# Gated cross-attention and mixture block: value diagonals copied in four steps, another softmax order, six score banks in batch 0

## The chip, the cores and the metric

The kernel runs on one core of a Trainium2 chip. The metric is the device time of one execution in microseconds (us), as the median of several runs. All data is float32.

## The reference

A decoder block works on x, of shape 8 batches x 256 tokens x 512, and on a context of the same shape.

```python
x = x + tanh(g_xattn) * attention(layernorm(x), context)      # 32 heads of 16, 8 key/value heads
x = x + tanh(g_ffn)   * feed_forward(layernorm(x))            # 128 experts, 4 chosen, plus a shared one
```

In the attention the queries come from the context and x together (1024 to 512). There are two sets of keys and values, one from the context and one from x, each with 8 heads. A token sees the 64 latest positions in each set, with a linear bias by distance and one softmax over both sets. A projection Wo follows.

In the feed-forward part all experts share 8 basis networks (512 to 256, silu(gate) * up). An expert is a mixture of them by its amplitudes, so that a token needs the 8 basis results, weighted by coefficients from the 4 experts that its router chose, then one product with w_down. A shared network of width 512 is added.

## The kernel before, in words

**Work and stages.** A batch has 256 tokens, two tiles of 128. Four kinds of work exist for each batch b, each a Python generator: `project(b)` (queries, keys, values; `project_first` for batch 0), `attention(b)`, `tail(b, t)` (Wo, layer norm, router, for token tile t) and `feed_forward(b)`. The code of all engines is emitted in one order: `run` (L1076) always resumes the generator whose planned time is earliest, and a `yield c` moves it on by c times a rate. Each engine, and each DMA queue, then executes its share strictly in the order of emission. In the middle of the run the feed-forward of batch b lies beside the attention of b+1 and the projection of b+2. Batch 0's attention has no feed-forward beside it, only `project(1)`.

**Attention.** `attention(b)` (L499) works on 8 groups i of two query blocks of 32 tokens; step u = 2i + j is block j of group i. `score(i)` (L515) writes the scores of group i into four PSUM banks, one for each pair p of key/value heads, by 8 matmuls. A bank has 512 columns: 192 for j = 0, 192 for j = 1, and the last 128 for results of `values`. At each step u, VectorE runs `soften` for the four pairs (bias and row minimum, L540), ScalarE the exponentials (L554), then, a step later, `divide` (reciprocal on VectorE, L563, scaling on GpSimd, L566), and two steps later `turn` transposes the probabilities (L574). `values(m, s, ...)` (L579) multiplies the probabilities of four steps with the values; it runs at the two steps of groups 3, 5, 7 and 9, right behind the scores, and writes into the last columns of the banks of pairs 0 and 1 of that same group. `take` (L609) copies them out on ScalarE. The work of a step is emitted in three pieces with a `yield` between them (L652): pair 0, pair 1, then pairs 2 and 3.

**Banks.** Of the eight PSUM banks, `ps_sc` has four in rotation (scores), `ps_gu` three, named gu0, gu1 and gu2 (feed-forward, by `next_bank`, in rotation), and `ps_one` one. `tail` uses `ps_one` once the feed-forward of batch 0 has been started, and `next_bank` before that.

**Values and diagonals.** `put_values` (L411) copies the values of a batch to `vpad`. For `values` they must stand in blocks on the diagonals of `vbd`. This is done by 16 DMAs of 128 KB on the queue of SyncE (SP), L628 to L634, all emitted at the start of step u = 3 for batch 0 and of step u = 1 for the others.

**The SP queue.** SP also issues nearly all other transfers, in order: x and the context of the batch after next (L105, L111), and the feed-forward weights (`load_gu`, L286). In batch 0 the feed-forward forms sums and differences of the weights (`sub`, L801: L805 and L807 on VectorE, L809 and L810 on GpSimd) and stores them in HBM (`keep`, L812, L814), from where later batches read them. In iteration k of the eight basis networks, each weight block for k + 2 is loaded as soon as the matmuls that used its buffer are emitted (`after`, L308). Differences of iteration k + 1 are formed in iteration k.

Of the kernel before, what the change touches and what calls it, by code (L numbers as in the profile page):

```python
# [36 lines left out]
def gated_block(  # L37
# [41 lines left out]
    def next_bank(name):  # L79
        turns[0] += 1  # L80
        return ps_gu.tile([P, 2, T], F32, tag=f"gu{turns[0] % 3}", name=name)

# [243 lines left out]
    def project_first():  # L328

        xt, ctT = loaded[0]  # L330
        xnT = two.tile([P, NC, T], F32, tag="xo", name="xnT_0")
        kT = two.tile([P, 2, 2, T], F32, tag="kT", name="kT_0")
        qT = two.tile([P, NB, G, Q], F32, tag="qT", name="qT_0")
        tiles = [slice(t * P, (t + 1) * P) for t in range(NT)]

        def early(name, parts):
            bank = ps_sc.tile([P, 512], F32, tag="sc", name=name)
            return bank.rearrange("p (a n) -> p a n", a=parts)

        def keys(pk, s, cols):  # L340
            w_sb, src = ((wsk_sb, ctT), (wk_sb, xnT))[s]
            for c in range(NC):
                nc.tensor.matmul(
                    pk[:, s, cols], lhsT=w_sb[:, c, :], rhs=src[:, c, cols],
                    start=(c == 0), stop=(c == NC - 1),
                )

        def put_keys(pk, s, cols):
            for par in range(2):
                nc.scalar.activation(  # L350
                    kT[:, par, s, cols], pk[:, s, cols], AF.Copy, scale=kmask[:, par : par + 1]
                )

        def queries(pq, g, cols, cs):
            for c in cs:
                nc.tensor.matmul(
                    pq, lhsT=wq_sb[:, c, g * P : (g + 1) * P],
                    rhs=(ctT if c < NC else xnT)[:, c % NC, cols],
                    start=(c == 0), stop=(c == 2 * NC - 1),
                )  # L360

        def put_queries(pq, g, t):
            blocks = slice(t * NB // NT, (t + 1) * NB // NT)
            nc.scalar.activation(
                qT[:, blocks, g, :], pq.rearrange("p (b q) -> p b q", q=Q), AF.Copy, scale=-0.25
            )

        pk = early("pk_0", 2)
        keys(pk, 0, slice(0, T))
        pqs = [next_bank(f"pq_0_{g}")[:, 0, :P] for g in range(G - 1)]  # L370
        pqs.append(ps_one.tile([P, P], F32, tag="one", name="pq_0_3"))
        for g in range(G):
            queries(pqs[g], g, tiles[0], range(NC))
        put_keys(pk, 0, slice(0, T))
        transposed(xnT, first_normed[0], 0, "x0", lambda shape, name: early(name, NC))()
        keys(pk, 1, tiles[0])
        for g in range(G):
            queries(pqs[g], g, tiles[0], range(NC, 2 * NC))
        put_keys(pk, 1, tiles[0])
        for g in range(G):  # L380
            put_queries(pqs[g], g, 0)
        projected[0] = kT, qT
        yield 0.0
        evict = transposed(
            xnT, first_normed[1], 1, "x0",
            lambda shape, name: next_bank(name).rearrange("p t (a n) -> p (t a) n", n=P),
        )
        yield 0.5
        evict()
        pk = next_bank("pk_0_1")  # L390
        keys(pk, 1, tiles[1])
        yield 0.6
        put_keys(pk, 1, tiles[1])
        pv = next_bank("pv_0").rearrange("p t (s n) -> p t s n", s=2)
        for t in range(NT):
            for s, (w_sb, src) in enumerate(((wsv_sb, ctT), (wv_sb, xnT))):
                for c in range(NC):
                    nc.tensor.matmul(
                        pv[:, t, s, :], lhsT=src[:, c, tiles[t]], rhs=w_sb[:, c, :],
                        start=(c == 0), stop=(c == NC - 1),  # L400
                    )
            yield 1.0
        put_values(pv)
        ready.add("values")
        for g in range(G):
            pq = next_bank(f"pq_0_{g}_1")[:, 0, :P]
            queries(pq, g, tiles[1], range(2 * NC))
            yield 1.0
            put_queries(pq, g, 1)

    def put_values(pv):  # L411
        nc.scalar.copy(
# [86 lines left out]
    def attention(b):  # L499
# [11 lines left out]
        def seen(row, qb):  # L511

            return row.rearrange("p (s k) -> p s k", s=2)[:, :, max(0, NW - 1 - qb) * Q :]

        def score(i):  # L515

            par, qb0 = groups[i]
            scs = [
                ps_sc.tile([P, 2 * COLS + P], F32, tag="sc", name=f"sc_{b}_{i}_{p}")
                for p in range(NPAIR)  # L520
            ]
            for j in range(2):
                qb = qb0 + j
                first = max(0, qb - NW + 1)
                for p in range(NPAIR):
                    rows = slice(32 * p, 32 * (p + 1))
                    nc.tensor.matmul(  # L527
                        seen(scs[p][:, j * COLS : (j + 1) * COLS], qb),
                        lhsT=qT[rows, qb].rearrange("p g q -> p (g q)"),
                        rhs=kT[rows, par, :, first * Q : (qb + 1) * Q],  # L530
                        start=True, stop=True,
                    )
            return scs
# [86 lines left out]
        prs, dens, pts = {}, {}, {}  # L620
        for u in range(2 * n + 4):
            i, j = divmod(u, 2)
            if u == (1 if b > 0 else 3):
                while "values" not in ready:
                    yield 0.2


                for qd in range(P // Q):  # L628
                    for g in range(G):
                        at = D * (1 - g % 2)  # L630
                        nc.sync.dma_start(
                            vbd[g * Q : (g + 1) * Q, qd].rearrange("p a k r -> p a (k r)"),
                            vpad[qd * Q : (qd + 1) * Q, :, at : at + 2 * HK * D],
                        )  # L634
            m = i // 2 - 1 if i >= 3 and i % 2 else None
            if j == 0:
                if i < n:
                    scs = score(i)
                elif m is not None:
                    scs = [  # L640
                        ps_sc.tile([P, 2 * COLS + P], F32, tag="sc", name=f"sc_{b}_{i}_{p}")
                        for p in range(2)
                    ]
            if m is not None:
                values(m, j, pts[m], scs)
            exponentials()
            if i < n:
                prs[u] = three.tile([P, NPAIR, COLS], F32, tag="pr", name=f"pr_{b}_{u}")
                nmax = small.tile([P, NPAIR], F32, tag="nmax", name=f"nm_{b}_{u}")
                dens[u] = small.tile([P, NPAIR], F32, tag="den", name=f"dn_{b}_{u}")  # L650
            yield 1.0
            for step, ps in enumerate(((0,), (1,), (2, 3))):  # L652
                exponentials()
                for p in ps:
                    if i < n:
                        soften(i, j, p, scs, prs[u], nmax, dens[u])
                if step == (0 if b > 0 else 1) and 0 <= u - 1 < 2 * n:
                    divide((u - 1) // 2, (u - 1) % 2, prs[u - 1], dens.pop(u - 1))
                if step == (1 if b > 0 else 2) and 0 <= u - 2 < 2 * n:
                    k = (u - 2) // 4  # L660
                    if (u - 2) % 4 == 0:
                        pts[k] = two.tile(
                            [P, P // Q, NPAIR, COLS], F32, tag="pt", name=f"pt_{b}_{k}"
                        )
                    turn(u - 2, prs.pop(u - 2), pts[k])
                if step == 1 and j == 1 and m is not None:
                    take(m, scs)
                    if m == n // 4 - 1:
                        start(tail(b, 0, oT), 0.30 if b > 0 else 0.22, total=37.0)
                if u < 2 * n + 2:  # L670
                    yield 1.0 if i < n else 0.8
# [22 lines left out]
    def tail(b, t, oT):  # L694
# [1 line left out]
        mine = []  # L696

        def take_bank():
            mine.append("fed" in ready)
            if mine[-1]:  # L700
                yield from hold()

# [4 lines left out]
        def bank(shape, name):  # L707
            if mine[-1]:
                return ps_one.tile(shape, F32, tag="one", name=name)
            flat = next_bank(name).rearrange("p a n -> p (a n)")[:, : prod(shape[1:])]  # L710
            return flat.rearrange("p (a n) -> p a n", a=shape[1]) if len(shape) == 3 else flat

        n = f"{b}_{t}"
# [443 lines left out]
```

## Time and profile before

| what | value |
|---|---|
| median of 3 runs (lowest, highest) | 1052.18 us (1050.83, 1053.58) |
| profiled execution, its own time | 1053.74 us |
| its span in the profile | 1051.8 us |
| TensorE (PE) busy | 1002.5 us, 95% |
| PE weight loads busy | 797.0 us, 76% |
| VectorE (DVE) busy | 583.4 us, 55% |
| ScalarE (ACT) busy | 422.6 us, 40% |
| GpSimd (POOL) busy | 428.6 us, 41% |
| DMA traffic | 177.13 MB, mean 168 GB/s |

The profile is one execution. Views used below: the busy time of each engine in chosen stretches of the span, with the TensorE clock that was granted (1.00 is full speed) and the share of the DMA engines in use; the waits, which say who waited for whom; and the timeline of one engine, in which a bracket at the end of a line gives the idle time ahead of the instruction and what ended it. On the SP queue's timeline an entry is the issue of a transfer, not its landing. A count of PE matmuls in the trace is twice that of the program, since a float32 matmul shows as two.

### The profile page before, as it was taken

Reading aid. Unit: us, or ns where it says so; the run is one execution under the profiler, and the core shown is the slowest. Engines: PE = TensorE matmul, PEld = TensorE weight load, DVE = VectorE, ACT = ScalarE, POOL = GpSimd, SP = SyncE. Lnnn points to the kernel's source line nnn. Section 1 sums busy time; section 2 is a strip of 40 time slices with the busy share of each in tenths; the row PEclk is TensorE's granted clock in tenths of the full one; section 3 lists DMA queues with packets and bytes.
Section 4 is the critical chain, followed back from the end, with each engine's and each line's share of the span. In section 5 each row is a group of like instructions: output and inputs, shape, how many; then the busy total and the mean of one; then the engine's idle time right before and its main releaser. Section 6 shows DMA issues by size and latency. Waiting matters only on the chain.

```text
span 1051.8 us, 26704 instructions
## 1 busy us (share of the span) xinstructions
PE 1002.5 (95%) x10072; PEld 797.0 (76%) x10072; DVE 583.4 (55%) x2193; ACT 422.6 (40%) x1608; POOL 428.6 (41%) x844
## 2 busy tenths in 40 slices
PE   6779959999999999999999999999999999999998
PEld 5656848786878778886878868787787868777885
DVE  1554657656754465635755367554665457654452
ACT  3542425425643255423644155432554236531220
POOL 3333558623643145531654136441455215640340
PEclk9879989999999999999999999999999999999999
DMA  8700685537745485436844387453864457653780
GB/s 251 196 15 4 173 257 160 169 99 210 249 135 158 122 264 177 141 112 175 279 128 162 101 227 227 129 170 107 257 193 132 129 155 236 193 172 111 260 281 20
DMA packets 109856, 177.13 MB, mean 168 GB/s; under 512 B 11936, under 2 KB 34976, under 8 KB 109728
## 3 DMA queue, kind: packets, MB, share of 16 engines
q1 hardware_dynamic: 107616, 173.59, 54.2%
q10 hardware_dynamic: 2112, 1.84, 0.5%
q8 instruction: 79, 1.29, 0.5%
q14 instruction: 49, 0.40, 0.1%
HBM read 146.02 MB, written 12.58 MB: 151 GB/s over the span
## 4 chain that ended last, share of the span: by engine, by line
PE 78%; DVE 6%; issue 2%; ACT 1%; ACTq 0%; DVEq 0%
PE m L857 30%; PE ps L991 11%; PE pq L469 8%; PE pd L1054 5%; PE sc L596 5%; PE po L721 5%; PE sc L527 4%; PE pd L1037 3%; PE pv L489 2%; PE pk L450 2%; DVE pr L540 1%; PE pl L752 1%; DVE pt L574 1%; DVE st_a L150 1%; ACT pr L554 1%
## 5 line engine op out<-in xcount | busy, mean ns | idle before, releaser
L566 POOL TENSOR_SCALAR pr<-pr,rd 128x192 f32<-128x192 f32 (+2 forms) x512 | 209.3, 427 | 301.6 <-DVE rd L563 301.6
L554 ACT ACTIVATE pr<-pr,nm 128x192 f32<-128x192 f32 (+2 forms) x512 | 218.6, 430 | 141.1 <-DVE nm L540 80.0
L857 PE MATMUL m<-w,sT 128*128 128x256 f32 x1024 | 254.2, 382 | 11.4 <-DVE th L825 11.4
L540 DVE CUSTOM_DVE_ANT_1 pr<-sc,nbias 128x192 f32<-128x192 f32 (+2 forms) x512 | 153.5, 322 | 158.3 <-PE sc L596 84.5
L857 PEld LDWEIGHTS m<-w,sT 128*128 128x128 f32 x1024 | 195.4, 192 | 38.9 <-DVE th L825 11.8
L857 PE MATMUL m<-w,hT 128*128 128x256 f32 x768 | 204.1, 388 | 0.0
L857 PEld LDWEIGHTS m<-w,hT 128*128 128x128 f32 x768 | 139.9, 191 | 24.5 <-issue 5.6
L930 POOL TENSOR_TENSOR mixed<-mixed,th 128x256 f32<-128x256 f32 x112 | 82.2, 734 | 161.5 <-DVE th L925 155.5
L991 PE MATMUL ps<-hT,w 128*128 128x256 f32 x512 | 117.6, 381 | 0.0
L574 DVE STREAM_TRANSPOSE pt<-pr 128x768 f32<-128x768 f32 (+2 forms) x128 | 111.5, 871 | 3.4 <-POOL prob L761 2.8
L991 PEld LDWEIGHTS ps<-hT,w 128*128 128x128 f32 x512 | 95.2, 190 | 14.6 <-issue 2.9
L554 ACT ACTIVATION_READ_ACCUMULATOR pr<-pr,nm 128x1 f32 x512 | 97.6, 191 | 0.0
L596 PEld LDWEIGHTS sc<-pt,vbd 64*32 64x32 f32 x5120 | 60.6, 106 | 24.6 <-issue 15.1
L527 PE MATMUL sc<-kT,qT 32*128 32x192 f32 (+2 forms) x1024 | 68.5, 343 | 7.9 <-DVE nm L540 4.8
L596 PE MATMUL sc<-pt,vbd 64*32 64x96 f32 (+2 forms) x5120 | 68.8, 228 | 5.5 <-DMA vbd<-vpad 3.3
L527 PEld LDWEIGHTS sc<-kT,qT 32*128 32x128 f32 x1024 | 48.9, 188 | 29.5 <-issue 8.6
L893 POOL TENSOR_TENSOR m<-m,u 128x256 f32<-128x256 f32 x64 | 47.3, 739 | 58.6 <-DVE u L892 50.4
L820 ACT ACTIVATE th<-m 128x256 f32<-128x256 f32 x64 | 24.6, 385 | 98.1 <-DVE up L903 98.1
L469 PE MATMUL pq<-ctT,wq 128*128 128x256 f32 x224 | 55.9, 394 | 3.1 <-ACT kT L457 2.9
L721 PE MATMUL po<-wo,oT 128*128 128x512 f32 x128 | 58.2, 597 | 0.0
L915 DVE TENSOR_TENSOR gate<-u,m 128x256 f32<-128x256 f32 x64 | 26.2, 409 | 55.0 <-PE m L857 55.0
L469 PE MATMUL pq<-xnT,wq 128*128 128x256 f32 x224 | 54.9, 389 | 0.0
(130 smaller groups left out, 1179.8 us busy)
## 6 DMA issues: line engine op xcount, KB each, us to landing
w<-s SPq DMA_DIRECT2D x224, 256.0 KB, 3.2
w<-in_L_ffn_w_gate SPq DMA_DIRECT2D x128, 256.0 KB, 3.0
w<-in_L_ffn_w_up SPq DMA_DIRECT2D x72, 256.0 KB, 3.9
vbd<-vpad SPq DMA_DIRECT2D x128, 128.0 KB, 3.0
s<-w SPq DMA_DIRECT2D x32, 256.0 KB, 3.3
w<-in_L_ffn_shared_w_gate SPq DMA_DIRECT2D x32, 256.0 KB, 3.1
w<-in_L_ffn_shared_w_up SPq DMA_DIRECT2D x32, 256.0 KB, 2.8
ctT<-in_ctx SPq DMA_DIRECT2D x8, 512.0 KB, 5.8
```

The source lines that it names most:

```text
L469: nc.tensor.matmul(pq, lhsT=wq_sb[:, c, g * P : (g + 1) * P], rhs=(ctT if c < NC else xnT)[:, c % NC, :], start=(c == 0), stop=(c == 2 * N ...
L527: nc.tensor.matmul(seen(scs[p][:, j * COLS : (j + 1) * COLS], qb), lhsT=qT[rows, qb].rearrange("p g q -> p (g q)"), rhs=kT[rows, par, :, f ...
L540: nc.vector.tensor_tensor_reduce(out=part, in0=seen(scs[p][:, j * COLS : (j + 1) * COLS], qb0 + j), in1=bass.AP(tensor=bias.tensor, offset ...
L554: nc.scalar.activation(part, part, AF.Exp, bias=nmax, scale=-1.0, accum_out=den)
L566: nc.gpsimd.tensor_scalar(part, part, rden[:, p : p + 1], 1.0, op0=ALU.mult, op1=ALU.mult)
L574: nc.vector.transpose(pt[:, u % 4].rearrange("p c (s k) -> p (c s) k", s=2)[:, :, lo:], pr.rearrange("p c (s k) -> p (c s) k", s=2)[:, :, ...
L596: nc.tensor.matmul(scs[gp][32 * c : 32 * (c + 1), 2 * COLS + lo * Q : 2 * COLS + hi * Q], lhsT=vbd[rows, kb % (P // Q), kb // (P // Q) * 2 ...
L721: nc.tensor.matmul(po, lhsT=oT[:, ch // 2, ch % 2, t * P : (t + 1) * P], rhs=wo_sb[:, ch % 2, ch // 2, :], start=(ch == 0), stop=(ch == 3),)
L857: nc.tensor.matmul(dst, lhsT=sides_of[m][c], rhs=w[:, c, :], start=(first and c == 0), stop=(c == NC // 2 - 1), skip_group_check=True,)
L930: nc.gpsimd.tensor_add(mixed[t], mixed[t], th)
L991: nc.tensor.matmul(pg[:, j, :], lhsT=w[c // 2][:, c % 2, ic % 2 * P : (ic % 2 + 1) * P], rhs=hT[:, c, :], start=(c == 0), stop=(c == NC - 1),)
L1054: nc.tensor.matmul(po, lhsT=lhsT, rhs=rhs, start=False, stop=(j == len(inner) - 1))
```

## The change

Four things change.

1. The 16 diagonal copies become a function, `diagonals(qd)`, of four DMAs. Batch 0 calls it four times directly behind `put_values`. The other batches call it once in each of four places: at the first and second piece of steps u = 1 and u = 2.
2. A step treats its pairs in the order 2, 3, then 0 and 1. The scores are computed in the same order of pairs.
3. From group 4 on, batch 0's scores rotate over six banks: the four of `ps_sc`, gu0 and gu1. The first four groups, and all groups of other batches, keep the four.
4. Batch 0's tails, where they used `next_bank`, use one fixed bank: gu2 for token tile 0 and gu0 for tile 1.

```diff
+    def other_bank(n, name):
+        return ps_gu.tile([P, 2 * T], F32, tag=f"gu{n}", name=name)
...
         put_values(pv)
-        ready.add("values")
+        for qd in range(P // Q):
+            diagonals(qd)
         for g in range(G):
...
+    def diagonals(qd):
+        for g in range(G):
+            at = D * (1 - g % 2)
+            nc.sync.dma_start(
+                vbd[g * Q : (g + 1) * Q, qd].rearrange("p a k r -> p a (k r)"),
+                vpad[qd * Q : (qd + 1) * Q, :, at : at + 2 * HK * D],
+            )
...
+        taken = [0]
+        def bank(name):
+            taken[0] += 1
+            if b == 0 and taken[0] > 4 * NPAIR and taken[0] % 6 < 2:
+                return other_bank(taken[0] % 6, name)
+            return ps_sc.tile([P, 2 * COLS + P], F32, tag="sc", name=name)
+
         def score(i):
...
-            scs = [
-                ps_sc.tile([P, 2 * COLS + P], F32, tag="sc", name=f"sc_{b}_{i}_{p}")
-                for p in range(NPAIR)
-            ]
+            scs = [bank(f"sc_{b}_{i}_{p}") for p in range(NPAIR)]
...
-                for p in range(NPAIR):
+                for p in (2, 3, 0, 1):
...
-            if u == (1 if b > 0 else 3):
-                while "values" not in ready:
-                    yield 0.2
-                for qd in range(P // Q):
-                    for g in range(G):
-                        at = D * (1 - g % 2)
-                        nc.sync.dma_start(
-                            vbd[g * Q : (g + 1) * Q, qd].rearrange("p a k r -> p a (k r)"),
-                            vpad[qd * Q : (qd + 1) * Q, :, at : at + 2 * HK * D],
-                        )
...
-            for step, ps in enumerate(((0,), (1,), (2, 3))):
+            for step, ps in enumerate(((2,), (3,), (0, 1))):
+                if b > 0 and u in (1, 2) and step < 2:
+                    diagonals(2 * (u - 1) + step)
...
-            mine.append("fed" in ready)
+            mine.append(b > 0 or "fed" in ready)
...
-            flat = next_bank(name).rearrange("p a n -> p (a n)")[:, : prod(shape[1:])]
+            flat = other_bank(2 - 2 * t, name)[:, : prod(shape[1:])]
```

## The prediction

> **What bounds the kernel now.** First the busy time by stretch of the span (columns: PE, PE weight loads, DVE, ACT, POOL busy us with counts; granted clock; DMA share; GB/s):
>
> ```profile
> 40.00:60.00 20.00, 12.33 (x242) 9.19 (x242) 8.77 (x46) 9.12 (x40) 6.66 (x18) 0.66 0.64 193
> 60.00:80.00 20.00, 15.97 (x179) 10.81 (x185) 11.30 (x46) 9.49 (x39) 7.44 (x17) 0.83 0.04 15
> 80.00:100.00 20.00, 17.73 (x403) 13.68 (x389) 8.85 (x36) 6.23 (x26) 7.74 (x15) 0.91 0.01 3
> ...
> 120.00:140.00 20.00, 14.76 (x85) 11.73 (x83) 10.44 (x43) 8.58 (x36) 12.49 (x20) 1.00 0.83 217
> 140.00:160.00 20.00, 12.59 (x180) 10.23 (x181) 14.57 (x56) 8.42 (x36) 13.21 (x21) 0.75 0.79 270
> ...
> 200.00:300.00 100.00, 99.56 (x1152) 78.67 (x1151) 61.20 (x242) 45.58 (x179) 41.72 (x86) 1.00 0.60 184
> ```
>
> From 200 to 900 us PE is busy 696.6 of 700 us at full clock: nothing but less PE work could shorten it. Time can be won only ahead of 160 us, where PE idles and then works at a lower clock: in batch 0's attention (40 to 108 us) and in one hole at 134 us. The waits of PE from 18 to 165 us (total, times, longest) name the causes:
>
> ```profile
> PE m L857 <- DVE th L825: 11.4, 1, 11.4
> PE sc L527 <- DVE nm L540: 3.5, 5, 1.1
> PE sc L596 <- DMA vbd<-vpad: 3.3, 3, 1.4
> PE pq L469 <- ACT kT L457: 2.9, 1, 2.9
> PE sc L527 <- ACT oT L613: 2.7, 1, 2.7
> ...
> PE sc L596 <- DVE rrd L767: 2.1, 1, 2.1
> ```
>
> The first is the hole. Three timelines show what stands behind it and behind the chain of batch 0. DVE:
>
> ```profile
> 44.96 0.36 DVE L540 CUSTOM_DVE_ANT_1 pr<-sc,nbias 128x192 f32<-128x192 f32 x1 [4.97 <-PE sc L596]
> ...
> 59.88 0.36 DVE L540 CUSTOM_DVE_ANT_1 pr<-sc,nbias 128x192 f32<-128x192 f32 x1 [3.98 <-PE sc L596]
> ...
> 144.30 0.69 DVE L807 TENSOR_TENSOR w<-w,w 128x512 f32<-128x512 f32 x1 [11.58 <-issue]
> ```
>
> The softmax of pair 0 waits for the values matmuls (L596) in its bank, and pairs 2 and 3, which need only scores, stand behind it. The third line is DVE waiting for a weight; POOL's wait beside it (9.5 us for the w_up load) names it. The SP queue tells why that is late:
>
> ```profile
> 121.76 0.33 SPq L300 DMA_DIRECT2D w<-in_L_ffn_w_up  x1
> 122.18 11.54 SPq L631 DMA_DIRECT2D vbd<-vpad  x16
> 133.77 0.59 SPq L105 DMA_DIRECT2D x<-in_x  x1
> 134.40 0.49 SPq L111 DMA_DIRECT2D ctT<-in_ctx  x1
> ...
> 137.93 0.84 SPq L300 DMA_DIRECT2D w<-in_L_ffn_w_up  x1
> ```
>
> The load at 137.93 (block 4, iteration 3) lands 6.3 us later, by the DMA view of that microsecond, and releases L807 at 144.3. Last, PE near the end of batch 0's attention:
>
> ```profile
> 91.83 0.80 PE L596 MATMUL sc<-pt,vbd 64*32 64x96 f32 x48 [2.08 <-DVE rrd L767]
> 92.56 3.44 PE L469 MATMUL pq<-xnT,wq 128*128 128x256 f32 x8
> ```
>
> Behind a 2.1 us gap eight records take 3.44 us that take 1.73 us elsewhere.
>
> **Part by part.** The yields that count stay the same, so the order of emission changes only inside steps.
>
> *Copies, batch 0: nothing.* SP already waits 11.0 us for `vpad`, its next entry; the copies start at 30.6 us when ACT has written it and still do. The 3.3 us wait of PE for `vbd` stays. No other entry of SP is overtaken: the weight loads are emitted later in both.
>
> *Copies, batch 1: -2 us.* The 16 copies keep 0.6 to 0.72 us of SP each, 11.5 in all. Where do the four groups fall? DVE's order gives the places: first pieces of steps 1 and 2 at 121.65 and 124.69, second pieces at 122.33 and 125.37. The feed-forward's step that emits the late load also emits the product L925 at 126.54, behind all four. So everything ahead of the load at 137.93 stays ahead: 16 copies, x, context, two loads and three stores; only two loads and three stores come sooner than before, with slack anyway. What changes is the mixture. Before, copies come first, then about 2.3 MB in one burst whose members take 4 to 6.6 us to land; after, copies come just ahead of the load. From 122 to 144 us the DMA share averages 0.86, so of these 22 us at most 0.14, 3.0 us, is free for better packing. Bounds 0 and -3.0; I take -2, since SP's copies alone leave the DMA share at 0.7 (128 to 132 us), the slack that loads between them fill. Next late is the same L807: the hole shrinks from 11.4 to about 9.4 us. The half-rate work behind it (eight records of L857 in 3.57 us, not 1.9) stays.
>
> *Copies, batches 2 to 7: 0.* They stand among loads for which PE did not wait even behind 16 in a row. The last group comes 1.5 steps later, but is needed at step 6; at about 5 us per step that is 17 us, against 3.0 us to land.
>
> *Pairs 2 and 3 first, batch 0.* Prices: a softmax with its accumulator 0.275 us, reciprocal 0.1, transpose 0.97, exponentials 0.55 a pair. I follow the chain:
> - Steps 6 and 7: pairs 2 and 3 (0.55) run in the 4.97 us wait. POOL's division of step 5 starts at 40.7, not 45.8, so the coefficients (L264), which waited 1.1 us for POOL's earlier work, no longer do. Step 7 ends on DVE at 48.9, not 50.55: -1.65. The copies oT come 1.7 us sooner and with them the score of group 4, the keys' matmul (54.4) 2.0 us sooner.
> - Step 10: behind the values' end DVE has two pairs and a transpose (1.5), not four, a reciprocal and the transpose (2.15): -0.65, together -2.65. ACT's kT follows, so its 2.9 us wait stays and moves along.
> - Steps 14 and 15: DVE, from the values' end, 2.75 before and 1.6 after, as two pairs and a weight difference move ahead. POOL's division of step 14 starts before values, about 81.0, not 84.97. Behind it stand the two weight differences on POOL (2.6) and the division of step 15. So the last transpose goes from 90.80 to 86.8: -4.0.
> - The 2.08 us gap above becomes about 1.0; if the eight records then run at full clock, that is a further 1.7. Together about 5.5 us.
>
> Here a rule weighs against me. The Trainium skill (*TensorE: Matmul & The Clock Gate*, "Why this matters for your kernels") has the clock fall only when PE pauses more than about 3 us; by it a 2.1 us gap costs no clock, closing it wins none, and the sum is 3.8. The row says otherwise: 3.44 for 1.73, with the clock at 0.73 from 90.5 to 94 us. I follow the row.
>
> *Six banks and fixed tail banks: +0.5 us, already taken off the 5.5.* *Perfetto Trace Analysis* of the skill ("Matmuls") says that rotating through more banks overlaps emptying with the next matmuls; by it the 2.7 us (L613) and 1.1 us waits of scores would go. Counting allocations six back, a group's pairs 2 and 3 get the banks of the former group's pairs 0 and 1, which now empty last, and the score begins with 2 and 3. PE takes its matmuls in order, so only pair 2 of group 4 is free early. At group 7 the score starts behind the third softmax rather than the first: +0.55. Bounds: -3.8 by the rule, +0.55 for each of three groups; I take the nearest row's wait, group 7's. Tail steps already follow one another, so one bank costs them nothing; the feed-forward's first banks are free by then (last tail reads by 107.7, second bank first needed at 111.9).
>
> *Pair order, batches 1 to 7: 0.* DVE waited 65.6 us for L596 from 200 to 900 us, yet PE lost only 3.4 us to everything there: that bounds a gain. A loss would be a reciprocal that now meets unfinished exponentials ahead of a feed-forward operation on DVE, at most 1 us each and hidden while PE has queued matmuls.
>
> **Sum.** 1053.74 (its own time; span 1051.8 plus 1.9 around) - 5.5 - 2 = 1046.2. The median of the runs lies 1.56 below that execution, so 1044.7.
>
> **Rivals.**
> - *The hole stays whole*: DMA bandwidth rather than order sets the landing. Only batch 0's gain: 1052.2 - 5.5 = 1046.7. For it: share 0.9 and more from 134 to 140 us.
> - *The hole closes*: should the late load stand ahead of the last eight copies, 5.8 us fall away, and with an earlier neighbour landing sooner perhaps all 11.4 and 1.7 at half rate: 1052.2 - 18.6 = 1033.6. Against it: DVE's order, L925 behind step 2.
> - *Given back*: PE is in order, and slower clock windows absorb the gain in batch 0 (PE has 42.7 us of full-clock work in 68): 1050.5.
> - *Slower*: the bank order. If pairs 2 and 3 still wait for values, nothing of the 5.5 comes, but the score of groups 4 to 7 still begins with the banks emptied last: 4 x 0.55, and one more window at half rate, some 3 us of values and queries doubled: +5.2 - 2 = +3.2, 1055.4. It decides once the early softmax wins less than 2 us. For it: score rows already run at half clock (1.81, not 0.93, at 77.8).
>
> **Chances.** Forecast with 4 to 11 us gained 0.54; hole whole 0.16; hole closed 0.10; given back 0.12; slower 0.08. So faster 0.80, same 0.12, slower 0.08; 0.3%, 3.2 us, is about what a measurement of this kernel can tell from no change. Leaving out the closed hole and the slower case, the range reaches from 1038 (the forecast with the full 3.0, and with 5 of the 7 us spared that half rate costs from 45 to 71 us, where about 14 us of busy PE run at 0.5) to 1051.
>
> **What would show it.** First feed-forward matmul at about 103, not 108.4; L540 of step 6 starting near 40 without a wait on L596; last transpose of batch 0 near 87; 91.8's gap about 1 us and its query at 1.7 us. One hole of about 9 us on PE, ended by L807, with SP's late load still behind 16 copies. The 700 us in the middle still at 99.5%. Wrong if the hole is gone, if the score of groups 5 to 7 waits over 1.7 us, or if PE's idle time grows behind 200 us.

## The result, and the profile after

The changed kernel takes 1049.09 us (median of 9 runs, 1046.65 to 1050.84), the kernel before, run beside it, 1052.18 (9 runs; its medians beside the later experiments are 1053.18 to 1053.46). The ratio is 0.996 with an interval of [0.9945, 0.9974]: about 4.2 us faster, between 2.7 and 5.8 (it compares means; the two medians lie 3.1 us apart). The forecast was 1044.7 with a range of 1038 to 1051. The range holds the time; the likeliest value was 4.4 us too low. The profiled execution after took 1049.43 us with a span of 1047.3, so 4.5 us of span against the one before.

The busy time by stretch (same columns as before):

```profile
40.00:60.00 20.00, 14.56 (x252) 10.94 (x235) 11.17 (x56) 10.78 (x47) 8.29 (x22) 0.66 0.62 192
60.00:80.00 20.00, 16.25 (x326) 11.56 (x326) 12.66 (x52) 10.82 (x43) 7.89 (x18) 0.91 0.04 15
80.00:100.00 20.00, 18.27 (x255) 13.52 (x255) 7.92 (x25) 3.55 (x16) 6.21 (x13) 0.91 0.01 2
...
120.00:140.00 20.00, 10.29 (x56) 8.38 (x56) 8.30 (x34) 5.77 (x24) 11.54 (x17) 0.89 1.03 285
140.00:160.00 20.00, 19.43 (x215) 15.39 (x216) 18.37 (x65) 11.75 (x47) 16.20 (x29) 0.77 0.58 188
...
200.00:900.00 700.00, 696.60 (x7203) 554.44 (x7202) 407.78 (x1568) 299.45 (x1157) 281.38 (x570) 1.00 0.56 173
```

From 40 to 100 us PE is busy 49.1 us, not 46.0, so batch 0 is denser. The hole now lies wholly in the stretch from 120 to 140. The DMA share there is 1.03, not 0.83, so the DMA engines have nothing free. The long middle is as full as it was. The waits of PE from 18 to 165 us:

```profile
PE m L865 <- DVE th L833: 10.1, 1, 10.1
PE sc L547 <- DVE nm L560: 3.6, 4, 1.8
PE sc L616 <- DMA vbd<-vpad: 3.4, 3, 1.4
...
PE pq L483 <- ACT kT L471: 2.0, 1, 2.0
PE sc L616 <- DVE rrd L775: 1.6, 1, 1.6
```

L865 is the former L857, L547 the former L527, L616 the former L596, L560 the former L540, L815 the former L807. The hole fell from 11.4 to 10.1 us, the wait for the keys from 2.9 to 2.0, and the wait of a score for oT (2.7) is gone. The longest score wait grew from 1.1 to 1.8. DVE's timeline, at the places shown before:

```profile
39.87 0.36 DVE L560 CUSTOM_DVE_ANT_1 pr<-sc,nbias 128x192 f32<-128x192 f32 x1
...
44.81 0.36 DVE L560 CUSTOM_DVE_ANT_1 pr<-sc,nbias 128x192 f32<-128x192 f32 x1 [4.21 <-PE sc L616]
...
137.94 0.69 DVE L815 TENSOR_TENSOR w<-w,w 128x512 f32<-128x512 f32 x1 [10.27 <-issue]
```

Pair 2 of step 6 starts at 39.87 without a wait; only pairs 0 and 1 stand behind the values. The SP queue ahead of the late load:

```profile
116.96 2.54 SPq L420 DMA_DIRECT2D vbd<-vpad  x4
119.54 0.60 SPq L108 DMA_DIRECT2D x<-in_x  x1
120.18 0.53 SPq L114 DMA_DIRECT2D ctT<-in_ctx  x1
...
122.26 2.82 SPq L420 DMA_DIRECT2D vbd<-vpad  x4
...
128.61 5.12 SPq L420 DMA_DIRECT2D vbd<-vpad  x8
133.77 0.59 SPq L303 DMA_DIRECT2D w<-in_L_ffn_w_up  x1
```

All 16 copies, x and the context still stand ahead of it. It is issued 4.2 us sooner than before (133.77 for 137.93), and L815 starts 4.2 us behind it, where it was 6.4. Last, PE at the end of batch 0 and behind the hole:

```profile
86.71 0.73 PE L616 MATMUL sc<-pt,vbd 64*32 64x96 f32 x48 [1.58 <-DVE rrd L775]
87.36 3.52 PE L483 MATMUL pq<-xnT,wq 128*128 128x256 f32 x8
...
140.57 3.78 PE L865 MATMUL m<-w,sT 128*128 128x256 f32 x8 [10.09 <-DVE th L833]
144.28 2.84 PE L547 MATMUL sc<-kT,qT 32*128 32x192 f32 x16
147.05 1.29 PE L616 MATMUL sc<-pt,vbd 64*32 64x96 f32 x64
```

The gap is shorter, 1.58 for 2.08 us, but the query behind it runs at half rate again. The 16 score records at 144.28 take 2.84 us; in the middle of the run they take 0.93.

Comparing the start of the same matmul in both traces gives the account of the gain:

| place (time before) | gain, us | what changed it |
|---|---|---|
| last values of batch 0 (91.83) | 5.12 | softmax order in batch 0 |
| first feed-forward matmul (108.36) | 5.05 | |
| end of the hole (146.92) | 6.35 | hole 1.30 shorter |
| a later feed-forward matmul (154.70) | 5.07 | half clock behind the hole lasts longer |
| keys of batch 2 (163.36) | 5.70 | a wait of 0.56 for xnT gone |
| 261.8 | 5.84 | |
| 385.3, 508.7, 632.2, 755.6 | 5.60, 5.48, 5.06, 4.89 | some 0.1 to 0.4 lost per batch |
| end | 4.54 | |

Each gain includes the 0.28 us by which the first work behind the initial loads (tr_x) came sooner in the trace after.

### The profile page after: what moved, and what is told of

It is laid out like the page before. It is cut to its first block, busy times and chain, and to the rows that moved or that the text cites. A ratio compares the mean times of both kernels' runs of the same rounds, so it can differ in the third digit from the quotient of the medians.

```text
span 1047.3 us, 26708 instructions
## 1 busy us (share of the span) xinstructions
PE 1003.2 (96%) x10072; PEld 798.4 (76%) x10072; DVE 586.0 (56%) x2193; ACT 420.6 (40%) x1608; POOL 427.5 (41%) x844
## 4 chain that ended last, share of the span: by engine, by line
PE 85%; DVE 7%; DMA 2%; issue 2%; ACT 2%; SPq 1%; POOL 1%; ACTq 0%; DVEq 0%
PE m L865 32%; PE ps L999 11%; PE pq L483 9%; PE sc L616 6%; PE pd L1062 5%; PE po L729 5%; PE sc L547 5%; PE pd L1045 3%; PE pk L464 3%; PE pv L503 2%; DVE pr L560 2%; PE pl L760 1%; ACT pr L574 1%; DMA wq<-in_L_xattn_Wq 1%; SPq L420 1%
## 5 line engine op out<-in xcount | busy, mean ns | idle before, releaser
L865 PE MATMUL m<-w,sT 128*128 128x256 f32 x1024 | 255.0, 384 | 10.1 <-DVE th L833 10.1
L865 PEld LDWEIGHTS m<-w,sT 128*128 128x128 f32 x1024 | 196.1, 192 | 37.5 <-DVE th L833 10.5
L560 DVE CUSTOM_DVE_ANT_1 pr<-sc,nbias 128x192 f32<-128x192 f32 (+2 forms) x512 | 153.7, 323 | 117.7 <-PE sc L547 103.4
L865 PE MATMUL m<-w,hT 128*128 128x256 f32 x768 | 204.2, 389 | 0.0
L865 PEld LDWEIGHTS m<-w,hT 128*128 128x128 f32 x768 | 140.2, 191 | 24.4 <-issue 5.6
L616 PEld LDWEIGHTS sc<-pt,vbd 64*32 64x32 f32 x5120 | 61.4, 107 | 25.1 <-issue 14.1
L616 PE MATMUL sc<-pt,vbd 64*32 64x96 f32 (+2 forms) x5120 | 69.6, 230 | 5.5 <-DMA vbd<-vpad 3.4
L547 PE MATMUL sc<-kT,qT 32*128 32x192 f32 (+2 forms) x1024 | 69.3, 349 | 5.3 <-DVE nm L560 5.0
L547 PEld LDWEIGHTS sc<-kT,qT 32*128 32x128 f32 x1024 | 49.5, 192 | 27.3 <-issue 8.9
L828 ACT ACTIVATE th<-gate 128x256 f32<-128x256 f32 x64 | 26.5, 415 | 85.2 <-DVE gate L923 85.2
```

Source lines behind the costliest of these rows:

```text
L547: nc.tensor.matmul(seen(scs[p][:, j * COLS : (j + 1) * COLS], qb), lhsT=qT[rows, qb].rearrange("p g q -> p (g q)"), rhs=kT[rows, par, :, f ...
L560: nc.vector.tensor_tensor_reduce(out=part, in0=seen(scs[p][:, j * COLS : (j + 1) * COLS], qb0 + j), in1=bass.AP(tensor=bias.tensor, offset ...
L616: nc.tensor.matmul(scs[gp][32 * c : 32 * (c + 1), 2 * COLS + lo * Q : 2 * COLS + hi * Q], lhsT=vbd[rows, kb % (P // Q), kb // (P // Q) * 2 ...
L865: nc.tensor.matmul(dst, lhsT=sides_of[m][c], rhs=w[:, c, :], start=(first and c == 0), stop=(c == NC // 2 - 1), skip_group_check=True,)
```

## The experiments

My theory after this comparison: the pair order in batch 0 is the whole gain. The four steps only move bytes about in front of a load that waits for DMA work, not for its place in the queue, and they cost each later batch a little. Rivals: the banks contribute; the steps contribute through the hole; the hole is a matter of order after all. "Hole" below is PE's wait at the place of 146.92 (L857 before), "first FF" the start of batch 0's first feed-forward matmul. The start of an execution varies: tr_x, the first work behind the initial loads, begins at 14.94 us in the trace of before and between 14.66 and 17.68 us in the others. So places are compared by gaps and durations more than by absolute time.

| run | median us (runs) | ratio to before, interval | hole us |
|---|---|---|---|
| before | 1052.18 (9) | 1 | 11.39 |
| after | 1049.09 (9) | 0.996 [0.9945, 0.9974] | 10.09 |
| 1 pair order alone | 1047.89 (5) | 0.9957 [0.9944, 0.997] | 10.64 |
| 2 four steps alone | 1053.08 (14) | 0.9997 [0.9988, 1.0007] | 9.68 |
| 3 banks alone | 1052.32 (13) | 0.9993 [0.9982, 1.0004] | 11.43 |
| 4 change, copies in a row | 1049.73 (7) | 0.9964 [0.995, 0.9977] | 10.76 |
| 5 change, copies at u = 3, 4 | 1081.87 (4) | 1.0276 [1.0257, 1.0295] | 1.81 |
| 6 change, early x and context | 1044.68 (5) | 0.9921 [0.9908, 0.9935] | 7.54 |
| 7 change without batch 1's copies | 1040.15 (1) | no interval | 1.00 |
| 8 change, batch 0 scores 0 to 3 | 1050.15 (1) | no interval | 11.12 |
| 9 run 6, copies in a row | 1044.64 (5) | 0.9914 [0.99, 0.9927] | 7.86 |
| 10 run 6, batch 1 one group per step | 1040.45 (4) | 0.9879 [0.9864, 0.9893] | 2.62 |
| 11 run 10 without early loads | 1042.15 (6) | 0.9901 [0.988, 0.9921] | 6.40 |

**1. The pair order alone**, on the kernel before:

```diff
-                for p in range(NPAIR):
+                for p in (2, 3, 0, 1):
...
-            for step, ps in enumerate(((0,), (1,), (2, 3))):
+            for step, ps in enumerate(((2,), (3,), (0, 1))):
```

> Only the order of pairs is changed in the kernel before (scores and softmax 2, 3, 0, 1); four score banks, tails as before, the 16 copies in a row. Theory of the forecast: the softmax of pairs 2 and 3 ahead of the values matmuls is what moves batch 0, so the first feed-forward matmul comes at 103.5 to 104.5 us (108.36 before, 103.31 with the whole change) and the hole stays 11.4 us. Rival, that the six banks are what frees batch 0: first feed-forward matmul at 106.5 or later. A second question: the whole change lost about 1.3 us between 260 and 1047 us, some 0.25 us per batch. If the pair order costs it, batches take 123.6 to 123.8 us here; if the copies do, 123.44 as before.

The ratio is that of the whole change. The first feed-forward matmul comes at 101.99 us, sooner than expected, and the hole is 10.64 us, not 11.4. The last values of batch 0 come 4.84 us sooner, and the lead at 147 us (5.23) is the lead at the end (5.25). A batch in the middle takes 123.43 us (378.98 to 502.41), as before. On PE's timeline the query behind the gap ran at full rate here:

```profile
86.99 0.73 PE L596 MATMUL sc<-pt,vbd 64*32 64x96 f32 x48 [1.36 <-DVE rrd L767]
87.65 1.99 PE L469 MATMUL pq<-xnT,wq 128*128 128x256 f32 x8
```

So the 1.45 us at this place (1.99 for 3.44) exist, and one execution gets them while another does not. Here they were lost again in batch 1, where a score waited 1.7 us, not 0.58, and ran at half clock:

```profile
118.61 1.79 PE L527 MATMUL sc<-kT,qT 32*128 32x192 f32 x12 [1.70 <-DVE nm L540]
```

The longest score wait in batch 0 is still 1.1 us and the wait for oT is gone: the pair order takes that wait away without any bank.

**2. The four steps alone**, on the kernel before: batch b > 0 calls `diagonals` as in the change.

```diff
-            if u == (1 if b > 0 else 3):
+            if u == 3 and b == 0:
...
+                if b > 0 and u in (1, 2) and step < 2:
+                    diagonals(2 * (u - 1) + step)
```

> Only the four steps of the copies, in the kernel before. Theory: the first feed-forward matmul stays at 108.4 us, the hole shrinks by about 1.3 us to 10.1, as in the whole change, since everything ahead of the late load stays ahead and the DMA engines are full. Rival (the steps are worth more, and the whole change hides it): hole under 9 us. If the copies in steps cost the 0.25 us per later batch (their waits stand one by one before the values matmuls), batches take 123.6 to 123.8 us here, not 123.44, and the time is the same as before within 0.1%.

No difference can be measured. The hole is 1.7 us shorter in the trace, but the way from its end to the gain table's next place (154.70) is 1.2 us longer at half clock, and 0.1 to 0.2 us go in most later batches. The first feed-forward matmul is at 111.51 us; 2.5 of the 3.1 us behind the expected place are a later start (tr_x at 17.47).

**3. The banks alone**, on the kernel before: `other_bank`, the rotation over six from group 4 on, and the fixed banks of the tails, with the old pair order.

```diff
+            if b == 0 and taken[0] > 4 * NPAIR and taken[0] % 6 < 2:
+                return other_bank(taken[0] % 6, name)
```

> Only the six banks for batch 0 and the fixed banks of its tails, with the pairs in their old order. Here a group's first two pairs get banks emptied two groups ago, so that its score can start early. Theory of the forecast: DVE still meets pair 0 first and waits for values, so little is won: first feed-forward matmul at 107 to 108.4 us. Rival (the banks free batch 0): 104 to 106 us. Hole 11.4 in both.

No difference can be measured either. The wait for oT is still 2.7 us and the wait for kT still 2.9. One wait does get shorter, that of group 7's score: four of its records find free banks, and the other twelve wait 0.62 us, where all 16 waited 1.14 before.

```profile
77.76 1.81 PE L527 MATMUL sc<-kT,qT 32*128 32x192 f32 x16 [1.14 <-DVE nm L540]
```
```profile
76.98 0.59 PE L536 MATMUL sc<-kT,qT 32*128 32x192 f32 x4
78.20 1.19 PE L536 MATMUL sc<-kT,qT 32*128 32x192 f32 x12 [0.62 <-DVE nm L549]
```

The gap at the end of the chain stays (2.10 us), and with it the time.

**4. The change with the copies in a row again**: batches 1 to 7 issue all 16 at the start of u = 1.

```diff
+            if b > 0 and u == 1:
+                for qd in range(P // Q):
+                    diagonals(qd)
...
-                if b > 0 and u in (1, 2) and step < 2:
-                    diagonals(2 * (u - 1) + step)
```

> The whole change, but with the 16 copies of batches 1 to 7 in a row at the start of step 1 as before. Theory: first feed-forward matmul at 103.3 as in the whole change, hole back to 11.4 us, so 1.3 us later behind it. If the steps cost 0.25 us per later batch, these come back here and the time equals that of the whole change within 0.5 us (1047 to 1048 of span); if the pair order costs them, it is 1.3 us slower than the whole change.

The time can't be told from that of the change. The trace is that of the fastest of seven executions: its first feed-forward matmul is at 100.17 us, not 103.3 as expected, and the hole is 10.76 us, not 11.4. The lead does not shrink in the later batches: 6.55 us at 163 and 6.50 at 828. So the slow loss of the change belongs to the steps. Most of it sits in one place, the first values of a batch. These are PE's lines there in batch 3, from three timelines: before, after, and this run:

```profile
384.30 1.03 PE L596 MATMUL sc<-pt,vbd 64*32 64x96 f32 x64
```
```profile
378.46 1.28 PE L616 MATMUL sc<-pt,vbd 64*32 64x96 f32 x64
```
```profile
377.79 1.02 PE L616 MATMUL sc<-pt,vbd 64*32 64x96 f32 x64
```

The same 64 records take 0.25 us longer when the copies were emitted in four groups, and no record waits visibly. From batch 3 to batch 7 these records take 1.13 to 1.28 us in the five traces with steps and 1.02 to 1.11 in the seven with the row (run 5 waits there). Yet on the SP queue the 16 copies stand back to back in both versions. Before and after, in batch 3:

```profile
362.49 11.05 SPq L631 DMA_DIRECT2D vbd<-vpad  x16
```
```profile
360.96 11.06 SPq L420 DMA_DIRECT2D vbd<-vpad  x16
```

What differs is the distance: the last issue ends 10.8 us ahead of the values before and 6.4 us after. Whether that, or the four groups themselves, makes the records longer, no run isolates.

**5. The copies later**, at u = 3 and 4, behind the late load:

```diff
-                if b > 0 and u in (1, 2) and step < 2:
-                    diagonals(2 * (u - 1) + step)
+                if b > 0 and u in (3, 4) and step < 2:
+                    diagonals(2 * (u - 3) + step)
```

> The whole change, with the four groups of copies two steps later: at steps u = 3 and 4 instead of 1 and 2, so that the late weight load stands ahead of all 16. Theory (the DMA engines are full, their share was 1.0 or more from 122 to 140 us with the change): the hole moves one iteration on, to the loads that are now behind the copies, and keeps 6 to 10 us in sum. Rival (the place of the copies ahead of that load makes the hole): PE waits under 3 us in sum from 120 to 160 us, and the time falls to about 1040 us.

Both expectations failed. From 120 to 160 us PE waits 10.1 us in sum, the theory's 6 to 10, but for the copies and not for weights. The hole at its old place nearly closes, 1.81 us, with a lead of 14.3 us there. But then the values wait for the copies in every batch. PE's waits from 100 us to the end:

```profile
PE sc L616 <- DMA vbd<-vpad: 28.7, 17, 3.3
```

PE is busy 677.4 us of the 700 in the middle, not 696.6, and behind each wait it runs at half clock for a while. The margin that my prediction worked out for the last group at u = 2, 17 us, was too large: in the later batches of the change the last issue ends 6.4 us ahead of the values (run 4). Two steps later nothing is left: in batch 2 the last group is issued at 256.22 us and the values start at 256.18.

**6. x and the context of batch 2 earlier**, about 1 MB less ahead of the late load: `project(2)` no longer loads them; SP issues them at 49.3 and 50.0 us, in batch 0's attention. With the change the DMA engines are full there to 50 us (share 0.99 from 45), then fall to 0.57 and from 55 us to 0.01, so that 1 MB more finds room.

```diff
+    def load_early():
+        loaded[2] = load(2), load_context(2)
...
-            loaded[b] = load(b), load_context(b)
+            if b > 2:
+                loaded[b] = load(b), load_context(b)
...
+        start(once(load_early), 1.0, at=-0.44)
```

> The whole change, with x and context of batch 2 (1 MB) loaded before batch 0's feed-forward, while the DMA engines are idle, and not beside the copies. Theory (DMA engines full): 1 MB took some 3 us of them, so the hole shrinks from 10.1 to 6.5 to 8 us and the time by 2 to 4 us. Rival (SP's issues bound the landing): two issues of 1.1 us in all fall away, the hole shrinks by 1.1 us at most.

Its ratio lies 0.4% below that of the change, some 4 us, at the upper end of the expected 2 to 4. PE's line at the end of the hole:

```profile
138.63 3.39 PE L869 MATMUL m<-w,sT 128*128 128x256 f32 x8 [7.54 <-DVE th L837]
```

The hole is 2.55 us shorter, and no copy stands elsewhere. At the 350 GB/s that the change moves between 122 and 126 us, 1 MB is an estimated 3.0 us. The rival, SP's two issues, allowed 1.1 us at most. The DMA work ahead of the load sets the hole.

**7. No copies in batch 1.** This leaves part of the computation out: batch 1 multiplies its probabilities with batch 0's values.

```diff
-                if b > 0 and u in (1, 2) and step < 2:
+                if b > 1 and u in (1, 2) and step < 2:
```

> The whole change without the 16 copies of batch 1; its attention then uses batch 0's values, so batch 1's output is another. Theory: the 11 us of DMA work fall away, the hole closes (PE waits under 1 us there) and with it the half clock behind it, so the feed-forward of batch 0 ends 11 to 13 us sooner. Rival (the hole is the feed-forward's own lack of DMA bandwidth in batch 0): a hole of 3 us or more stays.

```profile
130.38 2.00 PE L865 MATMUL m<-w,sT 128*128 128x256 f32 x8 [1.00 <-DVE th L833]
```

The hole is 1.0 us and the matmuls behind it run at full rate (2.00 us for 3.78). So nine of the ten us are the work of these 2 MB, and the 1 us gap itself does not cost the clock. But the score of batch 1 right behind these matmuls now waits 1.78 us, and from 134.8 to 141.6 us the clock is at half all the same.

**8. Batch 0's scores in the old order**, with the softmax order and the banks of the change:

```diff
-                for p in (2, 3, 0, 1):
+                for p in (0, 1, 2, 3) if b == 0 else (2, 3, 0, 1):
```

> The whole change, with batch 0's scores in the order of pairs 0, 1, 2, 3, so that the pairs whose banks were emptied two groups ago come first. Theory of the forecast (the first two matmuls of a score wait for the banks that empty last): the wait of PE for the score of group 7, 1.8 us with the change, falls to 0.9 to 1.3. Rival (the wait is for the last softmax in either order): it stays at 1.6 to 1.9.

The longest score wait falls from 1.76 to 1.2 us, by the 0.55 that the prediction had for the bank order, and group 4 waits 0.34. A gap nearer the end of the chain does not get shorter by it (1.61), and the time, a single run, shows nothing. The hole of this kernel, with the copies in four steps, is 11.12 us. Over all traces the copies in four steps give 10.09, 9.68 and 11.12 us, and those in a row 11.39, 10.64, 11.43 and 10.76. So of the 1.3 us that one pair of traces showed, some 0.75 is what the means differ by (10.3 and 11.05), less than either spread. Nor do the steps decide how long PE runs at half clock behind the hole:

| trace | copies in batch 1 | hole us | half clock behind it, us |
|---|---|---|---|
| before | row | 11.39 | 3.2 |
| run 1 | row | 10.64 | 4.5 |
| run 3 | row | 11.43 | 3.3 |
| run 4 | row | 10.76 | 11.8 |
| after | steps | 10.09 | 8.5 |
| run 2 | steps | 9.68 | 8.4 |
| run 8 | steps | 11.12 | 4.7 |

Run 4, then run 8, in the columns used above:

```profile
138.20:149.80 11.60, 11.60 (x97) 8.64 (x98) 10.03 (x38) 4.73 (x20) 9.36 (x19) 0.50 0.51 173
```
```profile
142.20:146.70 4.50, 4.50 (x12) 2.97 (x12) 4.40 (x18) 2.49 (x11) 4.50 (x11) 0.50 0.67 254
147.00:151.00 4.00, 4.00 (x85) 3.51 (x86) 4.00 (x12) 1.51 (x7) 1.83 (x3) 1.00 0.24 91
```

**9. Early loads and copies in a row**: runs 4 and 6 together.

> The changed kernel, but x and the context of batch 2 are loaded ahead of batch 0's values, and the copies of batches 1 to 7 stand in a row at u = 1. If the four steps cost the later batches some 0.15 to 0.25 us each, as the runs so far say, and the early loads are worth some 4 us, the two add up: the early loads' gain stays, the slip of 0.3 to 0.7 us behind 250 us goes, 1043 to 1044.5. If the row is dearer once the loads are gone (its 16 copies then stand alone, with DMA engines at 0.7), the hole is some 2 us longer than with four steps and early loads (7.5) and the time is 1046 or more.

The median is that of run 6, just above the expected 1043 to 1044.5. The trace has the hole at 7.86 us, so the row is not 2 us dearer, and the lead no longer slips (11.81 us at the end of the hole and at 828). The steps are worth nothing measurable with early loads either; that giving them up gains the slip back is in the trace but too small for the times.

**10. Batch 1's groups one step apart**, with the early loads, and a row in the later batches:

```diff
+            if b > 1 and u == 1:
+                for qd in range(P // Q):
+                    diagonals(qd)
...
-                if b > 0 and u in (1, 2) and step < 2:
-                    diagonals(2 * (u - 1) + step)
+                if b == 1 and u in (1, 2, 3, 4) and step == 0:
+                    diagonals(u - 1)
```

> The changed kernel with the early loads, copies of batches 2 to 7 in a row at u = 1, and batch 1's four groups one each at the first piece of u = 1, 2, 3 and 4, so that two groups are emitted behind the load that ends the hole. Theory of DMA work: 256 KB to 1 MB less stands ahead of that load, the hole falls from 7.5 to some 2 to 3 us, but the last group, some 3 us of copies, lands close to the values of u = 6: up to 3 us of waits for vbd and a stretch at half clock behind each; net 1041 to 1045. Rival: the values wait in batch 1 for every group, as in the run with copies at u = 3 and 4, and take all of it back: 1046 to 1050.

This is the fastest version that computes everything: 1040.45 us, a little below the expected 1041 to 1045 and as fast as the one run of the kernel that leaves batch 1's copies out (1040.15). Its SP queue and PE's line behind the hole:

```profile
122.32 3.03 SPq L420 DMA_DIRECT2D vbd<-vpad  x4
...
127.79 0.33 SPq L303 DMA_DIRECT2D w<-in_L_ffn_w_up  x1
128.17 2.54 SPq L420 DMA_DIRECT2D vbd<-vpad  x4
...
132.31 2.80 SPq L420 DMA_DIRECT2D vbd<-vpad  x4
```
```profile
132.94 2.94 PE L872 MATMUL m<-w,sT 128*128 128x256 f32 x8 [2.62 <-DVE th L840]
135.80 3.69 PE L551 MATMUL sc<-kT,qT 32*128 32x192 f32 x16
```

Eight copies now stand ahead of the late load (127.79) and eight behind it. PE does not wait for `vbd` in batch 1 at all, so the last group still lands in time. The rival, waits in batch 1 as in run 5, falls. The half clock behind the hole did not go: it lasted from 133.8 to 144.1 us.

**11. The same without the early loads.**

> The kernel of the run before without the early loads of x and context: only the place of the copies differs from the changed kernel (batch 1 one group each at u = 1, 2, 3 and 4, batches 2 to 7 in a row). With the early loads the hole was 2.6 us; without them x and context (1 MB, some 2.5 to 3 us of full DMA engines) stand ahead of the late load again. Theory that DMA work ahead of the load sets the hole: about 5 to 6 us of hole instead of 10.1, and a median of 1043 to 1045. Rival: the place of the copies matters only together with the early loads, since the loads that then come between the copies push the last group against the values of u = 6, so that PE waits for vbd over 2 us and the median is 1047 to 1050.

1042.15 us, better than expected, with a hole of 6.40, a little longer than expected, and no wait for `vbd` in batch 1. Beside the change it has only other places for the copies. The two measures add up roughly: from 10.1 us of hole the later place takes 3.7, the early loads alone 2.55, both together 7.5, a little more than the sum.

## Why the prediction was right in sign and too large

**What was right.** The chain of batch 0 went as followed. Step 7 ended on DVE at 49.14 us (forecast 48.9), the keys' matmul came at 52.15 (52.4), the first feed-forward matmul at 103.31 (about 103). The copies' count ahead of the late load, the release by L815 and the full middle were as forecast. Run 1 shows that this order alone is the gain, run 3 that six banks bring nothing measurable, and run 8 that the bank order costs the 0.55 us named. From tr_x to the last values batch 0 takes 76.0 to 77.4 us in the three traces with the old softmax order and 70.2 to 72.5 in the ten with the new one, so this gain is far above the difference between executions. Run 8 is among the ten, so it is the softmax order, and the order of the scores isn't needed. From the skill's rule that matmul groups should rotate through different banks (*Perfetto Trace Analysis*, "Matmuls") the prediction had worked out up to 3.8 us for the banks alone; run 3 got 0.5 us at one score and nothing that the times can tell.

**Where two misses cancelled.** Of the 5.5 us in batch 0, 1.7 were to come from the clock behind the 2.08 us gap. In the profiled execution they did not come: gap 1.58, not about 1, and the query 3.52 us. The term is also too large: 1.73 us is the distance from start to start, while the line of a query at full clock shows 1.99, so 1.45 can be won. The chain itself won more than the 3.8 left: the last transpose came at 85.68, not 86.8, and the score of group 4 lost its whole 2.7 us wait, not only 1.7 of it. Together 5.05, of which 0.28 is the earlier start; that this is near 5.5 is luck. In runs 1, 4, 6, 7, 8, 9 and 10 the same query took 1.99 to 2.00 us, in runs 5 and 11 3.40 and 3.35, behind gaps that differ little. So this term varies from execution to execution, and no run shows what decides it. Behind the old gap of 2.08 to 2.10 us it took 3.44 to 3.55 in all three traces: that such a gap costs the clock was read rightly. The parts don't quite add up on paper either: 4.0 for the transpose and 1.7 for the clock are 5.7, not 5.5.

**The step that failed first: "Copies, batch 1: -2 us".** Run 2, the steps alone, shows no gain: 0.9997, with an interval from 1.3 us faster to 0.7 slower. I had taken -2 between 0 and -3.0 because 0.14 of the DMA share was free. The trace gave -1.30, and the seven traces of both arrangements differ by about 0.75 in the mean. The share rose to 1.0 and more from 122 to 140 us, so the work was packed tighter, as assumed. But against a batch that now comes 5.05 us sooner the load was issued 0.9 us late (4.16 us sooner), and only the quicker landing, 4.17 us for 6.37, made the hole shorter. I had also written that "the half-rate work behind it stays". In this pair of traces it grew: PE ran at 0.50 for 8.5 us behind the hole, to 149.1, where before it was 3.2 us. That took 1.28 us back, all of the hole's gain. But this isn't the steps' price: run 4 has 11.8 us of it with the row and run 8 only 4.7 with the steps (table at run 8). The prediction held fixed what varies between executions: 3.2 to 11.8 us of work at half rate, which is 1.6 to 5.9 us lost.

**The second: "Copies, batches 2 to 7: 0".** It was 0.1 to 0.25 us per batch from batch 3 on, at the first values (1.28 us for 1.03 in batch 3), some 0.65 us from 262 to 756. Another 0.3 us lost there is no part of it: a values group took 1.44 us for 1.16, as one does in traces with the row too (1.55 in run 1). I had asked only whether the copies land in time, and had the margin at 17 us where the last issue ends 6.4 us ahead of the values.

**The sum again.** 1053.74 - 5.05 (batch 0) - 1.30 (hole) + 1.28 (half clock) - 0.77 (a wait for xnT and rest to 262 us) + 1.30 (later batches and end) = 1049.20, against 1049.43 measured; the remaining 0.23 lies outside the span. The forecast for the same execution was 1046.2. The difference of 3.2 us is 0.45 in batch 0, the -2 that came to nothing, the 1.30 in the later batches and 0.23 outside the span, less the 0.77. The median was further off, by 4.4 us, since I carried over the 1.56 us by which the profiled execution of before lay above its median; that of after lay only 0.34 above.

**The rivals.** "The hole stays whole" (1046.7) was right in its mechanism, DMA work ahead of the load and not the order of that work; the time lies 2.4 us above its sum, that of run 1, without steps, 1.2. Run 6 (1 MB less ahead of the load, 2.55 us), run 7 (2 MB less, 9.1 us) and run 11 (two groups behind the load, 3.7 us) show it. "The hole closes" was right about what would close it, the late load ahead of the last eight copies: run 10 does that, with the early loads, and runs at 1040. The change doesn't put it there, as DVE's order said. "Given back" holds for the hole's part only: PE kept the 5 us of batch 0 to 146 us. "Slower" did not occur.

## What to carry to other kernels

Where a load stands behind a queue of transfers and the DMA engines are full, count the bytes ahead of it, and move those that nobody needs yet behind it or to an earlier, empty stretch; changing their order ahead of the load returned nothing measurable. Check the margin separately for each stage: the same copies two steps later cost 28.7 us of waits when every batch had them there, and nothing when only the batch with the hole had its last two groups there, one per step. A shorter stall counts as won only with the granted clock behind it counted too.

## What the runs showed of the hardware

**The clock behind short gaps.** Two traces show the same gap at the same place with both outcomes. PE in run 9 and in run 11:

```profile
85.07 0.73 PE L620 MATMUL sc<-pt,vbd 64*32 64x96 f32 x48 [1.58 <-DVE rrd L780]
85.73 2.00 PE L487 MATMUL pq<-xnT,wq 128*128 128x256 f32 x8
```
```profile
87.49 0.73 PE L616 MATMUL sc<-pt,vbd 64*32 64x96 f32 x48 [1.58 <-DVE rrd L778]
88.15 3.35 PE L483 MATMUL pq<-xnT,wq 128*128 128x256 f32 x8
```

At the hole, the eight records behind gaps of 1.00 and 1.81 us (runs 7 and 5) ran at full rate (2.00 and 1.99 us). Behind the gap of 2.62 us in run 10 they took 2.94 us, and half clock then went on while PE worked almost without a pause:

```profile
134.00:144.00 10.00, 9.92 (x93) 7.20 (x92) 8.88 (x31) 3.79 (x16) 7.75 (x17) 0.50 0.91 268
```

The Trainium skill (*TensorE: Matmul & The Clock Gate*, "Why this matters for your kernels") puts the limit at idle times of about 3 us. Here it lies lower and isn't fixed by the gap alone.

**Half clock comes in units of 3.41 us.** In all 13 traces each stretch at 0.50 that ends before the last matmuls lasts 3.41, 6.83, 10.24, 13.65 or 20.48 us: one, two, three, four or six times 3.41. Behind the hole, one execution therefore waits longer for the full clock than another. The stretch began in the hole (at 139.9 us before, at 135.5 after) and lasted three units before, four after and six in run 4. The length of the hole doesn't order these, as the table at run 8 shows, and no run shows what does. In batch 0 the units go with much of the 2 us by which executions with the new softmax order differ: ahead of the last values, the four traces at 70.2 to 71.2 us (runs 4, 7, 8 and 9) have three or four of them, the six at 71.8 to 72.5 have five.
